# K's weights in 128-byte runs turned by VectorE, new PSUM banks for the first step, and a reordered tail in a conditioned-attention kernel

## The chip, the cores and the metric

The kernel runs on one core of one Trainium2 chip. The metric is the device time of one execution in microseconds (us). TensorE (PE; its weight loads are shown as PEld), VectorE (DVE), ScalarE (ACT), GpSimd (POOL) and SyncE (SP) run side by side; here SP issues nearly all DMAs and ScalarE a few.

## The reference

The input x is 8 x 512 x 512 (batch, sequence, model width) and every batch has one conditioning row. There are 16 heads of 32. All is float32.

```python
Q = split_heads(x @ Wq.T + bq)          # K and V likewise
tQ = split_heads(tokens @ Wq.T + bq)    # tK likewise; tokens: one row per batch
scores = einsum('bhqd,bhkd->bhqk', Q + tQ, K + tK) / sqrt(32)
out = einsum('bhqk,bhkd->bhqd', softmax(scores), V)
return x + out.transpose(0, 2, 1, 3).reshape(B, S, 512)
```

## The kernel before, in words

**Steps.** A step `t` (0 to 31) is one batch and one group of four heads, 128 columns of the width. It has four stages, one per 128-row block `kc`. A stage of step t computes `exponentials(t, kc)`: TensorE puts minus the row maxima into four PSUM banks by a small bf16 matmul (L553) and adds the scores, keys in rows (L556), and ScalarE takes the exponential out of each bank (L567). The same stage computes scores, queries in rows, of one row block of the next step (`row_max`, L492). VectorE reduces their maxima (L483 for one head, L501 for two), and `denominators` (L511) lets ScalarE take exponentials of the same banks only to sum them. The rest of a stage is either half of a pair of projections of q, k or v for later steps (`first_products` and `other_products`, 7 products instead of 8 by combinations of 256-blocks, L396 and L399), or `weighted`, the values' product of the step before (L572). When all maxima of a step stand, `split_max` splits them into three bf16 parts (on GpSimd) and `transpose_max` turns them (L537) into `maxT`, which the next step's exponentials need.

**Banks.** PSUM has eight banks of 128 x 512. A row of `TURNS` says which bank each use of a stage takes: places 0 to 3 the exponentials, 4 to 7 the row maxima, and the projections a place that the exponentials have left. `advance` goes to the next row. Rows 0 to 7 repeat over the steps, 8 to 11 serve the last steps (`row(i)`), 12 to 16 the stages ahead of step 0. Step 0 uses rows 0 to 3.

**Order.** The order on each engine is that of the code (`manual_schedule`); DMAs of a queue go out in the order of the code as well. A DMA issue waits till its tile is free, and an instruction waits for the tiles that it reads.

**Start.** Four x tiles, Wq, Wk and Wv come in. Wq and Wk are loaded in rows (256 KB a piece, 2 KB a row) and turned by TensorE through PSUM (`transpose_w`, L259; copies L266 to L272). Wv is loaded in 16 pieces of 64 KB in runs of 128 bytes (`spread`, L215), placed so that VectorE's turn of 32 x 32 blocks (L713) completes the transpose. `project_qk_part` (L343) projects group 0 and 1 of q and k. `condition` (L650), `untranspose` (L637) and `condition_end` (L659, L665) make the conditioning rows `tok`, which `project_qk_end` adds (L356 for q on VectorE, L358 for k on ScalarE). GpSimd forms the combined blocks of weights (`combine_w`, L288 to L291). Then come five stages (rows 12 to 16) of row maxima for step 0 and the second pair of groups, then step 0.

**End.** Steps 29, 30 and 31 have no projections left. `part_of` computes part of a step's values product and stores or adds it in `parts` (L757 to L764). For steps 30 and 31 no separate denominators are computed: GpSimd and VectorE sum the exponentials in `acc` and `acc2` (`sum_of`, L834, L836), and `times_ones` (L582) sums over the rows on TensorE. `send` turns a result on VectorE (L628), GpSimd scales it and adds the residual (L629, L630), and SP stores it in four pieces (L633). The last step is turned by TensorE (L637, L941) and stored in two halves (L952), one by SP and one by ScalarE.

Of the kernel before, what the change touches and what calls it, by code (L numbers as in the profile page):

```python
# [17 lines left out]
def kernel(  # L18
# [84 lines left out]
    ]  # L103
    turn = [0]

# [6 lines left out]
        return psum[:, j : k + 1 : k - j, :]  # L112

    def advance():
        turn[0] = (turn[0] + 1) % 8 if turn[0] < 8 else turn[0] + 1

    count = [0]

# [16 lines left out]
    def spread(a, d):  # L135

        return a.rearrange("(f j) d -> j f d", j=BL)[:, :, d : d + BL]
# [67 lines left out]
    nc.scalar.dma_start(cond_sb[B : B + 1, :], bq.rearrange("(o d) -> o d", o=1))  # L205
    nc.scalar.dma_start(cond_sb[B + 1 : B + 2, :], bk.rearrange("(o d) -> o d", o=1))
    load_w("q", Wq, nc.sync, [0])
    load_w("k", Wk, nc.sync, [0])
    load_w("q", Wq, nc.sync, [1, 2, 3])
    load_w("k", Wk, nc.sync, [1, 2, 3])  # L210

    wv = ws["v"].rearrange("p c (f e) -> p c f e", e=BL)
    for cc in range(NC):
        for h in range(HG):
            nc.sync.dma_start(  # L215
                wv[h * BL : (h + 1) * BL, cc], spread(Wv, cc * P + h * BL)
            )
    bvb = const.tile([P, D], F32, tag="bvb", name="bvb")
    nc.sync.dma_start(bvb, bv.rearrange("(o d) -> o d", o=1).broadcast_to([P, D]))
    bvs = const.tile([P, G, BL], F32, tag="bvs", name="bvs")  # L220
# [31 lines left out]
        n: const.tile([P, NC, D], F32, tag=f"wT{n}", name=f"wT_{n}") for n in ("q", "k", "v")  # L252
    }

    def transpose_w(n, dc, pt, odd=None):

        odd = dc % 2 if odd is None else odd
        for cc in range(NC):
            nc.tensor.transpose(  # L259
                pt[:, cc * P : (cc + 1) * P], ws[n][:, dc, cc * P : (cc + 1) * P], ident  # L260
            )
        o = wT[n][:, :, dc * P : (dc + 1) * P]
        pv = pt.rearrange("p (c s) -> p c s", c=NC)
        if n == "q":
            if odd:
                nc.vector.tensor_scalar(o, pv, SCALE, None, ALU.mult)  # L266
            else:
                nc.scalar.activation(o, pv, AF.Copy, scale=SCALE)
        elif odd:
            nc.vector.tensor_copy(o, pv)  # L270
        else:
            nc.scalar.copy(o, pv)  # L272
# [202 lines left out]
    def row_max(t, qc):  # L475
        if t >= T:
            return
        open_max(t)
        for j in range(HG):
            row_scores(t, qc, j, banks(HG + j))  # L480
        if t < T - 2:
            for j in range(2):
                nc.vector.tensor_reduce(  # L483
                    nmax[t][:, qc, j : j + 1, 0], banks(HG + j), AX.X, ALU.max, negate=True
                )
        else:
            row_max_of(t, qc, 0, banks(HG, 2))
        row_max_of(t, qc, 1, banks(HG + 2, 2))
# [27 lines left out]
                accum_out=sums[t][:, qc, j, :],  # L516
            )

    def split_max(t):

        if t >= T:
            return
        m, sp = nmax[t], split[t % 2]
        rest = op.tile([P, NS, HG, 1], F32, tag="rest", name=f"rest_{t}")
        nc.gpsimd.tensor_copy(sp[:, :, :, 0:1], m)
        nc.gpsimd.tensor_tensor(rest, m, sp[:, :, :, 0:1], ALU.subtract)
        nc.gpsimd.tensor_copy(sp[:, :, :, 1:2], rest)
        nc.gpsimd.tensor_tensor(sp[:, :, :, 2:3], rest, sp[:, :, :, 1:2], ALU.subtract)

    maxT = {}  # L530

# [146 lines left out]
    for half in range(2):  # L678
        combine_x(0, half, nc.gpsimd)
    transpose_w("q", 0, bank(6), 1)  # L680
    transpose_w("k", 0, bank(3), 0)
    transpose_w("q", 1, bank(7), 1)
    pc = bank(5)
    BB = B + 2
# [13 lines left out]
    transpose_w("q", 3, bank(1), 1)  # L698
    for cc in range(NC):
        project_qk_part(0, "k", cc, pk)  # L700
    transpose_w("k", 1, bank(5), 0)
    condition("q", bank(6))
    transpose_w("k", 2, bank(3), 1)
    transpose_w("k", 3, bank(7), 0)
    condition_end("q", bank(1), nc.vector)
    project_qk_end(0, "q", pq)
    condition("k", bank(5))
    for cc in range(2):
        project_qk_part(1, "q", cc, bank(7))
    condition_end("k", bank(0), nc.gpsimd)  # L710
    project_qk_end(0, "k", pk)
    for cc in range(NC):
        nc.vector.transpose(wT["v"][:, cc, :], ws["v"][:, cc, :])  # L713
    for cc in range(2, NC):
        project_qk_part(1, "q", cc, bank(7))
    project_qk_end(1, "q", bank(7))
    for n in ("q", "k", "v"):
        combine_w(n)

    def nothing():  # L720
# [2 lines left out]

    turn[0] = 12
    row_max(0, 0)
    denominators(0, 0)
    project_qk(1, "k", banks(1))
    advance()
    row_max(0, 1)
    first_products("q", 0, 1, lambda: denominators(0, 1), nothing, 0, 1)  # L730
    advance()
    row_max(0, 2)
    other_products("q", 0, 1, lambda: denominators(0, 2), nothing, (0, 1))
# [8 lines left out]
    other_products("k", 0, 1, lambda: denominators(1, 0), nothing, (0, 2))  # L742
    turn_x(NC + 1)
    load_residual(0)
    turn[0] = 0


    parts = {}
# [28 lines left out]
    for t in range(T - 3):  # L777
        b, r = divmod(t, G)

        exponentials(t, 0)  # L780
        row_max(t + 1, 1)
        of = ((t - 1) // G + 1, (t - 1) % G)
        dens = lambda: denominators(t + 1, 1)
        if t:
            project_pair("q", *of, dens, nothing, 1 if r % 2 else (0, 3))
        else:
            first_products("v", 0, 0, dens, nothing, 3)
            turn_x(NC + 2)
            load_residual(1)
        turn_x(t + NC + 3)  # L790
        advance()

        exponentials(t, 1)
        row_max(t + 1, 2)
        dens = lambda: denominators(t + 1, 2)
        if t:
            dens()
            weighted(
                t - 1, banks(0), banks(1), lambda: combine_x(b + 1, r) if r < 2 else None
            )  # L800
        else:
            dens()
            other_products("v", 0, 0, nothing, nothing, (1, 0))
        advance()

        exponentials(t, 2)
        row_max(t + 1, 3)
        split_max(t + 1)
        dens = lambda: denominators(t + 1, 3)
        if t:  # L810
            project_pair("k", *of, dens, nothing, 1 if r % 2 else (0, 3))
        else:
            first_products("v", 0, 1, dens, nothing, 3)
            combine_x(1, 0)
        if t:
            load_residual(t + 1)
        advance()

        exponentials(t, 3)
        row_max(t + 2, 0)  # L820
        dens = lambda: denominators(t + 2, 0)

        def small():
            transpose_max(t + 1, banks(2 if r % 2 else 1))

        project_pair("v", *of, dens, small, 1 if r % 2 else (0, 2))
        advance()
# [44 lines left out]
    exponentials(t, 0)  # L872
    row_max(t + 1, 1)
    apart = masked(t - 1)
    part_of(t - 1, banks(0), [2])
    row(1)
    exponentials(t, 1)
    row_max(t + 1, 2)
    acc = room_for_sums(t)
    sum_of(t, acc, 1, nc.gpsimd)  # L880
    part_of(t - 1, banks(0), [3])
    spread_sums(apart, banks(1))
    den = denominators_of(t - 1, banks(1))
    row(2)
    exponentials(t, 2)
    row_max(t + 1, 3)
    split_max(t + 1)
    pa = banks(0)
    times_v(t, 0, pa)

    exponentials(t, 3, (1, 2, 3, 4))
    times_v(t, 1, pa)
    transpose_max(t + 1, bank(5), nc.vector.tensor_copy)
    times_v(t, 2, pa)
    for kc in (2, 3):
        sum_of(t, acc, kc, nc.vector)
    send_parts(t - 1, den)

    t = T - 1
    exponentials(t, 0, (6, 7, 1, 2))  # L900
    times_v(t - 1, 3, pa)
    exponentials(t, 1, (3, 4, 5, 6))
    pv = bank(7)
    times_v(t, 0, pv)
    exponentials(t, 2, (1, 2, 3, 4))
    times_v(t, 1, pv)
    pd = bank(5)
    times_ones(acc, pd, True, True)
    acc2 = room_for_sums(t)
    sum_of(t, acc2, 1, nc.vector)  # L910
    den = op.tile([P, NB, BL], F32, tag="dead", name=f"den_{t - 1}")
    nc.vector.transpose(den.rearrange("p f e -> p (f e)"), pd)
    rec = op.tile([P, NB, 1], F32, tag="recs", name=f"recs_{t - 1}")
    nc.vector.reciprocal(rec, den[:, :, 0:1])
    send(t - 1, pa, rec)
    exponentials(t, 3, (6, 1, 2, 3))
    times_v(t, 2, pv)
    pd = bank(4)
    times_ones(acc2, pd, True, False)
    times_ones([es[t, 2, pr] for pr in range(NP)], pd, False, False)  # L920
    times_ones([es[t, 3, pr] for pr in range(NP)], pd, False, True)
    times_v(t, 3, pv)

# [3 lines left out]
    two = [slice(0, HS), slice(HS, S)]  # L927
    nc.vector.tensor_copy(oT[:, two[0]], pv[:, two[0]])
    nc.scalar.copy(oT[:, two[1]], pv[:, two[1]])
    pi, po = bank(2), [bank(6), bank(1)]  # L930
    untranspose(den, pi)
    rec = op.tile([P, NS, HG, 1], F32, tag="rec", name="rec")
    nc.vector.reciprocal(
        rec, pi.rearrange("p (c h e) -> p c h e", c=NS, h=HG)[:, :, :, 0:1]
    )
    y = op.tile([P, NS, P], F32, tag="res", name="res")
    b, g = divmod(t, G)
    for i in range(2):
        cs = slice(i * 2, i * 2 + 2)
        for qc in (i * 2, i * 2 + 1):  # L940
            nc.tensor.transpose(  # L941
                po[i][:, qc * P : (qc + 1) * P], oT[:, qc * P : (qc + 1) * P], ident
            )
        nc.vector.tensor_tensor(
            y[:, cs].rearrange("p c (h e) -> p c h e", h=HG),
            po[i][:, two[i]].rearrange("p (c h e) -> p c h e", c=2, h=HG),
            rec[:, cs].broadcast_to([P, 2, HG, HD]),
            ALU.mult,
        )
        last = (nc.gpsimd, nc.vector)[i]  # L950
        last.tensor_tensor(y[:, cs], y[:, cs], xr[t][:, cs], ALU.add)
        (nc.sync, nc.scalar)[i].dma_start(  # L952
            out[b].rearrange("(c p) d -> p c d", p=P)[:, cs, g * P : (g + 1) * P], y[:, cs]
        )

# [30 lines left out]
```

## Time and profile before

| | before |
|---|---|
| runs | 734.62 us median of 3 (734.4 to 734.93) |
| profiled execution | 734.58 us, span of the instructions 732.6 us, granted TensorE clock 0.999 |
| TensorE busy | 725.0 us, 99% of the span |
| ScalarE, VectorE, GpSimd busy | 619.1, 530.4 and 183.2 us |
| DMA | 29.64 MB, mean 40 GB/s |

The time of the profiled execution is its span and about 2.0 us around it. Matmuls are pipelined and their ends are modelled, so a busy TensorE is not one at its peak. A row of a timeline gives start and length in us, the engine, the line, the operation, what it writes and reads, and in brackets how long the engine had been idle and what ended that. A row of the chain gives start, length and the work that the end of the program goes back to.

### The profile page before, as it was taken

How to read it: one execution, taken by the hardware profiler on the slowest of the kernel's cores; microseconds unless marked ns; L12 is line 12 of the kernel's file. 1: busy time of each engine (PE TensorE's matmuls, PEld its weight loads, DVE VectorE, ACT ScalarE, POOL GpSimd, SP SyncE). 2: the span in 40 equal slices, each digit the busy share in tenths (PEclk: the TensorE clock that was granted, in tenths of full speed). 3: DMA queues.
4: the chain of work that ended last, by engine and by line, in shares of the span. 5: the costliest groups of instructions: out<-in, count | busy, mean ns of one | idle time of the engine just before them, and what ended most of it. 6: DMA issues, size and time to landing. Idle time of an engine off the chain costs nothing.

```text
span 732.6 us, 15105 instructions
## 1 busy us (share of the span) xinstructions
PE 725.0 (99%) x5416; PEld 402.8 (55%) x5416; DVE 530.4 (72%) x845; ACT 619.1 (85%) x1542; POOL 183.2 (25%) x282
## 2 busy tenths in 40 slices
PE   9999999999999999999999999999999999999997
PEld 5466555565555565555565555565555566555432
DVE  3697776777767877777776877777767777767666
ACT  2478988989988988988989888988988989898665
POOL 3622221122221122221122221122221122221373
PEclk9999999999999999999999999999999999999999
DMA  8524211212211212221212221212110111110112
GB/s 220 87 44 73 45 30 30 44 30 46 44 31 29 44 30 44 45 33 27 45 29 45 44 36 24 45 30 44 30 24 8 30 29 30 30 26 7 27 15 44
DMA packets 202142, 29.64 MB, mean 40 GB/s; under 512 B 199370, under 2 KB 200394, under 8 KB 202068
## 3 DMA queue, kind: packets, MB, share of 16 engines
q1 hardware_dynamic: 201488, 28.01, 23.5%
q8 instruction: 42, 0.69, 0.4%
q10 hardware_dynamic: 580, 0.68, 0.3%
q14 instruction: 32, 0.26, 0.1%
HBM read 20.27 MB, written 8.39 MB: 39 GB/s over the span
## 4 chain that ended last, share of the span: by engine, by line
PE 97%; ACT 1%; DMA 1%; DVE 1%; issue 0%; SPq 0%; POOL 0%; DVEq 0%; POOLq 0%
PE psum L399 26%; PE psum L572 16%; PE psum L492 15%; PE psum L556 15%; PE psum L396 14%; PE psum L553 6%; PE psum L343 2%; PE psum L537 1%; DMA w_k<-in_L_cond_Wk_dram 1%; ACT e L567 1%; PE psum L259 0%; PE psum L582 0%; DVE nmax L501 0%; PE psum L650 0%; PE psum L603 0%
## 5 line engine op out<-in xcount | busy, mean ns | idle before, releaser
L511 ACT ACTIVATE dead<-psum,nmax 128x512 f32<-128x512 f32 x480 | 327.6, 703 | 5.6 <-DVE nmax L483 3.6
L567 ACT ACTIVATE e<-psum 128x512 f32<-128x512 f32 x512 | 264.5, 603 | 77.8 <-PE psum L556 77.7
L483 DVE TENSOR_REDUCE nmax<-psum 128x1 f32<-128x512 f32 x240 | 154.6, 686 | 143.7 <-PE psum L492 143.7
L501 DVE TENSOR_REDUCE nmax<-psum 128x2 f32<-128x1024 f32 x136 | 164.7, 1216 | 10.4 <-PE psum L492 9.1
L629 POOL TENSOR_TENSOR res<-res,recs 128x512 f32<-128x512 f32 x31 | 33.4, 1077 | 447.1 <-DVE res L628 447.1
L492 PE MATMUL psum<-kT,qT 32*128 32x512 f32 x1024 | 136.4, 601 | 0.0
L556 PE MATMUL psum<-qT,kT 32*128 32x512 f32 x1024 | 132.9, 588 | 0.0
L572 PE MATMUL psum<-e,v 128*32 128x512 f32 x1024 | 120.5, 597 | 0.0
L511 ACT ACTIVATION_READ_ACCUMULATOR dead<-psum,nmax 128x1 f32 x480 | 105.3, 219 | 0.0
L492 PEld LDWEIGHTS psum<-kT,qT 32*128 32x128 f32 x1024 | 57.7, 183 | 56.8 <-ACT dead L511 22.2
L572 PEld LDWEIGHTS psum<-e,v 128*32 128x32 f32 x1024 | 26.3, 110 | 65.3 <-issue 37.7
L553 PE MATMUL psum<-maxT,onesb 3*128 3x512 bf16 x512 | 52.5, 384 | 0.0
L556 PEld LDWEIGHTS psum<-qT,kT 32*128 32x128 f32 x1024 | 51.0, 185 | 2.5 <-issue 0.2
L396 PE MATMUL psum<-wc_v,xc 128*128 128x256 f32 x192 | 49.5, 380 | 0.5 <-ACT e L567 0.5
L553 PEld LDWEIGHTS <-onesb 3*128 3x128 bf16 x512 | 13.4, 90 | 61.6 <-issue 51.9
L399 PE MATMUL psum<-xc,wc_k 128*128 128x256 f32 x180 | 46.2, 379 | 0.0
L399 PE MATMUL psum<-xc,wc_q 128*128 128x256 f32 x180 | 46.2, 379 | 0.0
L169 POOL TENSOR_TENSOR xr<-xr,bvs 128x512 f32<-128x512 f32 x31 | 39.4, 1272 | 18.2 <-DMA xr<-in_x_dram 18.1
L630 POOL TENSOR_TENSOR res<-res,xr 128x512 f32<-128x512 f32 x31 | 40.3, 1301 | 2.4
L396 PEld LDWEIGHTS psum<-wc_v,xc 128*128 128x128 f32 x192 | 36.3, 190 | 6.1 <-ACT e L567 1.3
L396 PE MATMUL psum<-wT_v,xT 128*128 128x256 f32 x128 | 38.7, 405 | 0.0
L399 PEld LDWEIGHTS psum<-xc,wc_k 128*128 128x128 f32 x180 | 34.2, 190 | 4.6
(153 smaller groups left out, 773.7 us busy)
## 6 DMA issues: line engine op xcount, KB each, us to landing
xr<-in_x_dram SPq DMA_DIRECT2D x124, 64.0 KB, 2.5
out_dram<-res SPq DMA_DIRECT2D x124, 64.0 KB, 2.0
x<-in_x_dram SPq DMA_DIRECT2D x112, 64.0 KB, 2.4
w_q<-in_L_cond_Wq_dram SPq DMA_DIRECT2D x4, 256.0 KB, 4.5
w_k<-in_L_cond_Wk_dram SPq DMA_DIRECT2D x4, 256.0 KB, 4.4
w_v<-in_L_cond_Wv_dram SPq DMA_DIRECT2D x16, 64.0 KB, 3.3
x<-in_x_dram ACTq DMA_DIRECT2D x2, 256.0 KB, 4.1
x<-in_x_dram SPq DMA_DIRECT2D x2, 256.0 KB
```

The costliest lines, as they stand in the source:

```text
L169: nc.gpsimd.tensor_tensor(xr[t], xr[t], bias, ALU.add)
L396: nc.tensor.matmul(pt, xb, w, start=(kc == kcs[0]), stop=(kc == kcs[-1]))
L399: nc.tensor.matmul(pt, w, xb, start=(kc == kcs[0]), stop=(kc == kcs[-1]))
L483: nc.vector.tensor_reduce(nmax[t][:, qc, j : j + 1, 0], banks(HG + j), AX.X, ALU.max, negate=True)
L492: nc.tensor.matmul(pt, qkT["q", t][r, qc * P : (qc + 1) * P], qkT["k", t][r, :], start=True, stop=True,)
L501: nc.vector.tensor_reduce(nmax[t][:, qc, pr * 2 : pr * 2 + 2, 0], pt, AX.X, ALU.max, negate=True)
L511: nc.scalar.activation(dead, banks(HG + j), AF.Exp, bias=nmax[t][:, qc, j, :], accum_out=sums[t][:, qc, j, :],)
L553: nc.tensor.matmul(bank[j], onesb[r, :], maxT[t][r, :], start=True, stop=False)
L556: nc.tensor.matmul(bank[j], qkT["k", t][r, kc * P : (kc + 1) * P], qkT["q", t][r, :], start=False, stop=True,)
L567: nc.scalar.activation(e[:, i, :], bank[pr * 2 + i], AF.Exp)
L572: nc.tensor.matmul(pt[j * HD : (j + 1) * HD, :], vs[b % 2][:, kc, (g * HG + j) * HD : (g * HG + j + 1) * HD], es[t, kc, j // 2][:, j % 2, ...
L630: nc.gpsimd.tensor_tensor(y, y, xr.pop(t), ALU.add)
```

## The change

1. **K's weights.** Only K's first 128 rows are still loaded in rows, into a tile of their own (`wk0`), and turned by TensorE. The other 384 columns of the transposed K come in 16 pieces of 48 KB in runs of 128 bytes, ahead of V's 16 pieces in SP's queue, and VectorE turns them in four instructions of 128x384. TensorE's 12 transposes of K and their three copies go.
2. **q's second group** (group 1) is projected in pieces: one quarter after `condition("q")`, one after `condition("k")`, two later; before, two and two after `condition("k")`.
3. **V's turns.** VectorE turns one quarter of V where it turned all four; the other three follow the maxima of row block 0. GpSimd's combination of V comes after them, still behind q's and k's.
4. **Banks.** Step 0 gets rows of its own (17 to 20 of `TURNS`), reached by `advance`, which then goes on with row 4. Its first products use place 1 instead of 3, its other products places (0, 2) instead of (1, 0). In row 13 the first products of q use place 0 for the first and place 1 for the second product instead of the reverse.
5. **Tail.** Step 29's two last parts are computed together in the first stage of step 30, with one copy and one addition fewer. Step 30's first block goes to `parts` and the other three are added by VectorE, its `send` reads `parts`. The last split of maxima is done by VectorE, and the last row block reduces its first two heads singly. GpSimd sums only one half of the first two exponentials of step 30. `acc2` also takes in the third block of step 31, so one `times_ones` of four matmuls goes. The last result has a tile of its own, and both of its stores are issued by ScalarE.

```diff
+        (0, 1, 2, 3, 4, 5, 6, 7),
+        (2, 4, 3, 5, 0, 1, 6, 7),
+        (0, 1, 4, 5, 2, 3, 6, 7),
+        (2, 4, 3, 5, 6, 7, 0, 1),
...
-        turn[0] = (turn[0] + 1) % 8 if turn[0] < 8 else turn[0] + 1
+        turn[0] = {7: 0, len(TURNS) - 1: 4}.get(turn[0], turn[0] + 1)
...
-    load_w("k", Wk, nc.sync, [0])
+    wk0 = op.tile([P, D], F32, tag="dead", name="wk0")
+    nc.sync.dma_start(wk0, Wk[:P, :])
     load_w("q", Wq, nc.sync, [1, 2, 3])
-    load_w("k", Wk, nc.sync, [1, 2, 3])
-    wv = ws["v"].rearrange("p c (f e) -> p c f e", e=BL)
-    for cc in range(NC):
-        for h in range(HG):
-            nc.sync.dma_start(
-                wv[h * BL : (h + 1) * BL, cc], spread(Wv, cc * P + h * BL)
-            )
+    for n, w, f in (("k", Wk, HG), ("v", Wv, 0)):
+        wn = ws[n].rearrange("p c (f e) -> p c f e", e=BL)
+        for cc in range(NC):
+            for h in range(HG):
+                nc.sync.dma_start(
+                    wn[h * BL : (h + 1) * BL, cc, f:], spread(w, cc * P + h * BL)[:, f:]
+                )
...
-        if t < T - 2:
+        if t < T - 2 or t * NS + qc == T * NS - 1:
...
-    transpose_w("k", 1, bank(5), 0)
+    def turn_w(n, ccs, rows=slice(0, D)):
+        for cc in ccs:
+            nc.vector.transpose(wT[n][:, cc, rows], ws[n][:, cc, rows])
+
+    turn_w("k", range(NC), slice(P, D))
     condition("q", bank(6))
-    transpose_w("k", 2, bank(3), 1)
-    transpose_w("k", 3, bank(7), 0)
+    project_qk_part(1, "q", 0, bank(7))
     condition_end("q", bank(1), nc.vector)
     project_qk_end(0, "q", pq)
     condition("k", bank(5))
-    for cc in range(2):
-        project_qk_part(1, "q", cc, bank(7))
+    project_qk_part(1, "q", 1, bank(7))
     condition_end("k", bank(0), nc.gpsimd)
     project_qk_end(0, "k", pk)
-    for cc in range(NC):
-        nc.vector.transpose(wT["v"][:, cc, :], ws["v"][:, cc, :])
+    turn_w("v", [0])
...
-    for n in ("q", "k", "v"):
+    for n in ("q", "k"):
         combine_w(n)
...
     row_max(0, 0)
+    turn_w("v", [1, 2, 3])
+    combine_w("v")
...
-    first_products("q", 0, 1, lambda: denominators(0, 1), nothing, 0, 1)
+    first_products("q", 0, 1, lambda: denominators(0, 1), nothing, 1)
...
-    turn[0] = 0
+    advance()
...
-            first_products("v", 0, 0, dens, nothing, 3)
+            first_products("v", 0, 0, dens, nothing, 1)
...
-            other_products("v", 0, 0, nothing, nothing, (1, 0))
+            other_products("v", 0, 0, nothing, nothing, (0, 2))
...
-            first_products("v", 0, 1, dens, nothing, 3)
+            first_products("v", 0, 1, dens, nothing, 1)
...
-    part_of(t - 1, banks(0), [2])
+    part_of(t - 1, banks(0), [2, 3])
+    spread_sums(apart, banks(1))
+    den = denominators_of(t - 1, banks(1))
...
-    sum_of(t, acc, 1, nc.gpsimd)
-    part_of(t - 1, banks(0), [3])
-    spread_sums(apart, banks(1))
-    den = denominators_of(t - 1, banks(1))
+    sum_of(t, acc, 1, nc.gpsimd, [0])
+    part_of(t, banks(0), [0])
+    send_parts(t - 1, den)
...
-    split_max(t + 1)
-    pa = banks(0)
-    times_v(t, 0, pa)
+    split_max(t + 1, nc.vector)
+    pa, rest = banks(0), [1, 2, 3]
+    times_v(t, 1, pa, rest)
     exponentials(t, 3, (1, 2, 3, 4))
-    times_v(t, 1, pa)
+    times_v(t, 2, pa, rest)
     transpose_max(t + 1, bank(5), nc.vector.tensor_copy)
-    times_v(t, 2, pa)
-    for kc in (2, 3):
-        sum_of(t, acc, kc, nc.vector)
-    send_parts(t - 1, den)
+    sum_of(t, acc, 1, nc.vector, [1])
+    sum_of(t, acc, 2, nc.vector)
     t = T - 1
     exponentials(t, 0, (6, 7, 1, 2))
-    times_v(t - 1, 3, pa)
+    times_v(t - 1, 3, pa, rest)
+    nc.vector.tensor_tensor(parts[t - 1], pa, parts[t - 1], ALU.add)
+    sum_of(t - 1, acc, 3, nc.vector)
     exponentials(t, 1, (3, 4, 5, 6))
     pv = bank(7)
     times_v(t, 0, pv)
-    exponentials(t, 2, (1, 2, 3, 4))
+    acc2 = room_for_sums(t)
+    sum_of(t, acc2, 1, nc.vector)
+    exponentials(t, 2, (1, 2, 3, 0))
     times_v(t, 1, pv)
     pd = bank(5)
     times_ones(acc, pd, True, True)
-    acc2 = room_for_sums(t)
-    sum_of(t, acc2, 1, nc.vector)
+    sum_of(t, acc2, 2, nc.vector)
...
-    send(t - 1, pa, rec)
-    exponentials(t, 3, (6, 1, 2, 3))
+    send_parts(t - 1, den[:, :, 0:1])
+    exponentials(t, 3, (4, 6, 1, 2))
     times_v(t, 2, pv)
...
-    times_ones([es[t, 2, pr] for pr in range(NP)], pd, False, False)
...
-        (nc.sync, nc.scalar)[i].dma_start(
+        nc.scalar.dma_start(
```

More of the change, by code (lines that the diff above doesn't have):

```diff
@@ L253, with transpose_w @@
     }
-    def transpose_w(n, dc, pt, odd=None):
+    def transpose_w(n, dc, pt, odd=None, of=None):
         odd = dc % 2 if odd is None else odd
+        of = ws[n][:, dc, :] if of is None else of
         for cc in range(NC):
             nc.tensor.transpose(
-                pt[:, cc * P : (cc + 1) * P], ws[n][:, dc, cc * P : (cc + 1) * P], ident
+                pt[:, cc * P : (cc + 1) * P], of[:, cc * P : (cc + 1) * P], ident
             )
@@ L517, in denominators, with split_max @@
             )
-    def split_max(t):
+    def split_max(t, on=nc.gpsimd):
         if t >= T:
@@ L524, in split_max @@
         rest = op.tile([P, NS, HG, 1], F32, tag="rest", name=f"rest_{t}")
[L525 to L528, printed above, removed]
+        on.tensor_copy(sp[:, :, :, 0:1], m)
+        on.tensor_tensor(rest, m, sp[:, :, :, 0:1], ALU.subtract)
+        on.tensor_copy(sp[:, :, :, 1:2], rest)
+        on.tensor_tensor(sp[:, :, :, 2:3], rest, sp[:, :, :, 1:2], ALU.subtract)
     maxT = {}
@@ L680 @@
     transpose_w("q", 0, bank(6), 1)
-    transpose_w("k", 0, bank(3), 0)
+    transpose_w("k", 0, bank(3), 0, wk0)
     transpose_w("q", 1, bank(7), 1)
@@ L908 @@
     times_ones(acc, pd, True, True)
-    acc2 = room_for_sums(t)
-    sum_of(t, acc2, 1, nc.vector)
+    sum_of(t, acc2, 2, nc.vector)
     den = op.tile([P, NB, BL], F32, tag="dead", name=f"den_{t - 1}")
     nc.vector.transpose(den.rearrange("p f e -> p (f e)"), pd)
-    rec = op.tile([P, NB, 1], F32, tag="recs", name=f"recs_{t - 1}")
-    nc.vector.reciprocal(rec, den[:, :, 0:1])
-    send(t - 1, pa, rec)
-    exponentials(t, 3, (6, 1, 2, 3))
+    send_parts(t - 1, den[:, :, 0:1])
+    exponentials(t, 3, (4, 6, 1, 2))
     times_v(t, 2, pv)
-    pd = bank(4)
+    pd = bank(3)
     times_ones(acc2, pd, True, False)
-    times_ones([es[t, 2, pr] for pr in range(NP)], pd, False, False)
     times_ones([es[t, 3, pr] for pr in range(NP)], pd, False, True)
@@ L929 @@
     nc.scalar.copy(oT[:, two[1]], pv[:, two[1]])
-    pi, po = bank(2), [bank(6), bank(1)]
+    pi, po = bank(0), [bank(4), bank(6)]
     untranspose(den, pi)
@@ L935 @@
     )
-    y = op.tile([P, NS, P], F32, tag="res", name="res")
+    y = op.tile([P, NS, P], F32, tag="res_last", name="res", bufs=1)
     b, g = divmod(t, G)
```

## The prediction

> **What bounds the kernel now.** I read the busy shares first, then the chain that ended last, then the timelines of the first 48 us, of step 0 and of the last 25 us.
>
> ```profile
> span 732.6 us, 15105 instructions
> PE 725.0 (99%) x5416; PEld 402.8 (55%) x5416; DVE 530.4 (72%) x845; ACT 619.1 (85%) x1542; POOL 183.2 (25%) x282
> ...
> PE 97%; ACT 1%; DMA 1%; DVE 1%; issue 0%; SPq 0%; POOL 0%; DVEq 0%; POOLq 0%
> ```
>
> TensorE is the bound. From step 1 to step 28 nothing in the diff touches the order or the banks, so gains and losses arise before about 70 us and after about 699 us, and a shift made early carries through undamped. The chain, in order of time:
>
> ```profile
> 17.02 0.44 PE psum L259 x4
> 17.46 0.99 PE psum L650 x8
> 18.45 1.04 PE psum L259 x8
> ...
> 19.51 0.60 ACT wT_k L272
> ...
> 20.15 1.07 PE psum L650 x8
> 21.22 1.91 PE psum L343 x4
> 23.13 0.44 PE psum L637 x4
> 23.57 1.72 PE psum L343 x4
> 25.29 1.07 PE psum L492 x8
> ```
>
> See here that turning three quarters of K's weights (L259) costs TensorE 0.44 + 1.04 us, and that the condition product of K (L650 at 20.15) waits for ScalarE's copy of the last quarter.
>
> ```profile
> 31.51 1.13 PE L399 MATMUL psum<-xT,wT_q 128*128 128x256 f32 x4 [0.45 <-ACT kT L358]
> ...
> 51.19 1.13 PE L396 MATMUL psum<-wc_v,xc 128*128 128x256 f32 x4 [0.23 <-ACT e L567]
> ...
> 55.97 1.13 PE L396 MATMUL psum<-wT_v,xc 128*128 128x256 f32 x4 [0.31 <-ACT e L567]
> ```
>
> These timeline rows are almost all of TensorE's open waits: a bank that ScalarE still reads. And the source of the small pieces, and of the tail:
>
> ```profile
> 8.15 10.96 SPq L215 DMA_DIRECT2D w_v<-in_L_cond_Wv_dram  x16
> ...
> 23.89 2.49 DVE L713 STREAM_TRANSPOSE wT_v<-w_v 128x512 f32<-128x512 f32 x4
> ...
> 713.05 4.62 DVE L836 TENSOR_TENSOR acc<-acc,e 128x1024 f32<-128x1024 f32 x4
> ...
> 718.33 3.18 DVE L834 TENSOR_TENSOR acc<-e,e 128x1024 f32<-128x1024 f32 x2
> ```
>
> **Part 1, K turned by VectorE.** TensorE loses 12 transposes and ScalarE and VectorE lose three copies of some 0.6 us; VectorE gains four turns of 128x384, each three quarters of 2.49/4, so 0.47 us. TensorE's path from 17.02 was 8.27 us (the rows above). After, it is condition q 0.99, one quarter of q's second group (1.91 + 1.72)/4 = 0.91, untranspose 0.44, condition k 1.07, a quarter 0.91, untranspose 0.44, two quarters 1.72: 6.48. Gain 1.79; I take 1.7, as pieces restarted after a wait run a little longer.
>
> Condition: K lies turned when condition k is due, at 17.02 + 0.99 + 0.91 + 0.44 = 19.36, so its last piece must land by 19.36 - 0.47 - 0.1 = 18.8. SP issues 16 pieces where three 256 KB loads stood, from the same 6.48. The nearest row is V's: 10.96/16 = 0.685 us each, but 0.487 is the median of one issue, and the long ones (up to 1.53) mostly follow the three K loads that are now gone; the four bvs issues took 1.85, 0.46 each. So the last issue is between 6.48 + 0.83 + 14 x 0.5 = 14.3 (the second waits till 7.31, as its row did) and 6.48 + 15 x 0.685 = 16.8; landing takes 2.6 to 4.8, median 3.3. That is 16.9 to 21.6. I take 15 + 3.3 = 18.3, nearest to the medians: on time by 0.5. At 21.6, 2.8 us would be lost. What is queued behind these turns on VectorE: sum_q, tok, q's exit, sum_k, V's first turn, the row maxima; behind condition k on TensorE, everything.
>
> Here a rule speaks against the change. The Trainium skill, "DMA: Bandwidth & Descriptors", sections "Specifications" and "Rules for kernel authors", wants at least 512 B for line rate and says to coalesce small transfers; "Anatomy of one DMA" gives about 2.0 us fixed per DMA. One after another, 16 pieces would be an estimated 32 us, K would land near 38, and the kernel would be 20 us slower, at 754. The V row decides: 16 pieces of 128-byte runs were issued in 10.96 us with 2.6 to 4.8 us to landing each, so they overlap. A second rule, "VectorE: DVE Perf Modes", section "Rules for kernel authors", gives 128x128 transposes to TensorE where PSUM will do. In engine time that is right (1.48 against 1.88 us, and +0.4 if the engines were alike), but VectorE is idle from 14.4 to 19.15, with 4.8 before L270.
>
> **What is pushed back.** In SP's queue V's 16 pieces, bvb, bvs and the next batch's 16 x pieces start some 7 us later. V's last piece: 15.5 + 10.96 - 0.5 + 3.3 = 29.3 (ends 27 and 32.5). Its three late turns on VectorE (1.87 us) stand ahead of the maxima of row block 1, ready near 29.3. TensorE needs those banks only after 3.29 us of products, and a maximum plus exponential for two heads takes about 2.3 us, so up to about 1 us of lateness is hidden; at 32.5 some 2 us would not be. I take 0. x's pieces landed by 31.8 and are first turned at 43.87: 10 us of cover. GpSimd does wc_q and wc_k first (about 10 us from 22.6), so wc_v, now last, ends near 37.5 against 39.4 before, needed after 45. K's first quarter has its own tile, same size and place in the queue: 0.
>
> **Part 2, banks of the prologue and step 0.** First products of q go to bank 7, so the 0.45 wait on L358 falls: -0.45. Each stage of a step begins with L553, so the chain gives their lengths:
>
> ```profile
> 47.85 0.33 PE psum L553 x4
> ...
> 53.62 0.33 PE psum L553 x4
> ...
> 59.26 0.33 PE psum L553 x4
> ...
> 65.02 0.33 PE psum L553 x4
> ...
> 70.56 0.33 PE psum L553 x4
> ...
> 75.83 0.33 PE psum L553 x4
> ```
>
> Step 0 has 5.77, 5.64, 5.76 and 5.54 us. The next stage, with equal work, has 5.27 (70.56 to 75.83). Excess of the first three: 0.50 + 0.37 + 0.49 = 1.36. The new rows put the second product on the bank of the second exponential, not the fourth. What could be late next is ScalarE: 2.07 for the exponentials, 4 x 0.67 for the denominators, 0.4 for a copy, 5.2 of 5.27. I take -1.25; bounds -1.36 and -0.3.
>
> **Part 3, the tail.** TensorE does one times_ones less: -0.86. Two value products of step 29 move into one stage, which leaves its 3.6 us rhythm (scores 1.02, maxima 2.36 on VectorE) and grows by about 0.5; the last stage loses as much. Row maxima and split end where they did: maxima 0.5 later, four small VectorE instructions (0.2 each with their waits) for GpSimd's 1.27. Transposes of the maxima at 712.28 as before, but no product hides the copy after them: exps of step 31 start at 713.25 instead of 713.60, so -0.35. Then VectorE: nine adds at 4.62/4 = 1.14 (contended 1.6) and one of 0.65 from PSUM, in a row from 713.1, end at 724.0. The parts add waits for the last value product (715.4, done before its turn); behind it queue both accumulators. times_ones(acc2) is due at 722.9 and waits 1.1 us. So of 0.35 + 0.86 some 0.2 to 0.3 is left at TensorE's end. The normalised step 30 is then later: den, reciprocal and turn till 725.5, GpSimd 1.05 + 1.28 till 728.0, SP's four stores till 729.9, landing about 731.4; ScalarE's two stores go out at 729.05 and 729.5, one behind the other, against 729.64 for the last before. I take -0.2; bounds -0.9 (no wait on VectorE) and +0.6 (contended adds).
>
> **Sum.** -1.7 - 0.45 - 1.25 - 0.2 = -3.6 us. The profiled execution took 734.58 us (span 732.6 and 2.0 around it), 0.04 under the median of the runs, 734.62: 731.0.
>
> **Rivals.**
> A, slower: K's small pieces arrive late. It costs 1 us per us after 18.8, and turns the sum positive by 0.2% (1.5 us) from a landing at 23.9. If every piece took the long issue (the mean of the two longest neighbours, 0.96 and 1.53, is 1.25): last issue 25.2, landing 28.5, 9.7 lost, 740.7. For it: 128-byte runs moved at 76 to 126 GB/s in the windows from 12 to 20 us, against 351 to 388 from 6 to 10 us, where the big ones ran. Against it: no large loads lie ahead any more after 9.3. Chance 0.06.
> B, partly late: K or V by 1 to 3 us: 732 to 734. Chance 0.10.
> C, VectorE bounds the tail: contended adds as at 718.33 (1.59 each): tail +0.6, 731.8. For: ten instructions in a row. Against: GpSimd is idle then. Chance 0.12.
> D, the banks don't do it: ScalarE's 5.2 us stay the limit of step 0, only 0.3 gained: 732.0. Chance 0.10.
> Forecast: 0.62.
>
> **Numbers.** A measurement of this kernel can tell about 0.2% from no change, 1.5 us. Forecast, C and D lie wholly below 733.1, and half of B: 0.89 faster, 0.06 same, 0.05 slower, after a little of B and A goes to same. The range takes the forecast's bounds (-4.5) and goes up over C, D and the first half of B: 730.2 to 732.9.
>
> **What would show it.** Right: no L259 on K after 8.7 us, TensorE without a wait at condition k, row scores of block 0 near 23.6, the first L553 near 45.7, step 0's stages near 5.3, and a wait of times_ones on the accumulator near the end. Wrong: condition k or sum_q waiting on w_k's landing, maxima of block 1 behind V's turns with TensorE idle, or exponentials again ahead of products in step 0's chain.

## The result and the profile after

| | before | after |
|---|---|---|
| median of 9 runs | 734.93 us (734.4 to 736.12) | 732.68 us (732.33 to 734.05) |
| ratio | | 0.9974, 95% interval 0.9965 to 0.9982 |
| profiled execution | 734.58 us, span 732.6 | 734.05 us, span 732.3 |
| TensorE busy | 725.0 us | 722.3 us |

The kernel became faster by 2.25 us (by 1.94 against the 734.62 us from which the forecast started), where 3.6 were forecast. TensorE's busy time fell by 2.7 us, and its share of the span is still 99%. The profiled execution of after is one of two of the nine at 734.05, with a late start (the wait of 1.19 us below); the execution of the same kernel in the experiments (`again`, 732.62 us, span 730.8, a wait of 0.22) is nearer to the median, and the readings below use both.

The page and the chain of waits of after, in the order in which they were shown of before (start us, length us, work):

```profile
span 732.3 us, 15085 instructions
PE 722.3 (99%) x5396; PEld 401.8 (55%) x5396; DVE 535.7 (73%) x857; ACT 617.7 (84%) x1540; POOL 177.0 (24%) x276
```

```profile
9.16 1.19 issue
10.35 0.39 PE psum L693 x4
10.74 3.63 PE psum L350 x8
...
18.68 0.99 PE psum L657 x8
...
21.16 1.00 PE psum L657 x8
...
23.65 1.72 PE psum L350 x4
25.37 1.07 PE psum L499 x8
...
47.42 0.33 PE psum L560 x4
52.69 0.33 PE psum L560 x4
58.04 0.33 PE psum L560 x4
63.30 0.33 PE psum L560 x4
68.95 0.33 PE psum L560 x4
74.22 0.33 PE psum L560 x4
...
721.10 1.23 DVE acc L847
722.37 1.48 PE psum L589 x10
```

See four things. From the condition product of q (L657 at 18.68) to the first row scores (L499 at 25.37) the path is 6.69 us; before, from the transposes of K that stood at its head, it was 8.27, and 6.48 was forecast. K's condition product starts without a wait. The stages of step 0 are 5.27, 5.35, 5.26 and 5.65 us, where they were 5.77, 5.64, 5.76 and 5.54. In the tail, `times_ones` (L589) waits for VectorE's last addition to `acc2` (L847), as forecast. But the transposes of the condition rows (L693) start after a wait, which the profile before did not show. The timeline of VectorE has K's turns, on time, and the row of additions in the tail, without a gap and at the uncontended 1.14 us each:

```profile
15.96 2.03 DVE L711 STREAM_TRANSPOSE wT_k<-w_k 128x384 f32<-128x384 f32 x4
...
28.80 1.89 DVE L711 STREAM_TRANSPOSE wT_v<-w_v 128x512 f32<-128x512 f32 x3
31.16 1.29 DVE L490 TENSOR_REDUCE nmax<-psum 128x1 f32<-128x512 f32 x2 [0.48 <-PE psum L499]
...
717.69 2.35 DVE L845 TENSOR_TENSOR acc<-e,e 128x1024 f32<-128x1024 f32 x2
719.96 2.35 DVE L847 TENSOR_TENSOR acc<-acc,e 128x1024 f32<-128x1024 f32 x2
722.23 0.70 DVE L925 STREAM_TRANSPOSE den<-psum 128x512 f32<-128x512 f32 x1
```

So the engines did in the tail what was forecast: taken from the start of step 30, VectorE's last operation (L961) ends 0.2 us earlier than before. What comes behind it is the surprise. Before, the last two stores were issued at 729.35 and 729.64, and the span ended 3.0 us after the end of VectorE's last operation (729.61):

```profile
729.35 0.40 SPq L952 DMA_DIRECT2D out_dram<-res  x1
729.64 0.42 ACTq L952 DMA_DIRECT2D out_dram<-res  x1
...
out_dram<-res SPq DMA_DIRECT2D x1, 128.0 KB, 1.9
```

In after, the timeline, and behind it the view of the DMAs from 719 to 735 us in 40 slices of 0.4 us (busy tenths of the 16 engines, GB/s, then KB each and the median us from issue to landing), show the end like this:

```profile
726.37 2.04 SPq L640 DMA_DIRECT2D out_dram<-res  x4
...
727.07 0.63 DVE L961 TENSOR_TENSOR res<-res,xr 128x256 f32<-128x256 f32 x1
...
727.45 1.04 ACTq L962 DMA_DIRECT2D out_dram<-res  x2
```

```profile
DMA  0000000000000000000037777988900000000000
GB/s 0 0 0 0 0 0 0 0 0 0 0 0 0 0 0 0 0 0 0 0 54 109 119 109 119 269 130 171 245 7 0 0 0 0 0 0 0 0 0 0
...
out_dram<-res SPq DMA_DIRECT2D x4, 64.0 KB, 2.6
out_dram<-res ACTq DMA_DIRECT2D x2, 128.0 KB, 3.2
```

VectorE is done at 727.70 and the halves are issued at 727.45 and 727.98, but the second one (the trace has no landing of the first) lands 3.2 us after its issue instead of 1.9 to 2.0, and the span ends 4.6 us after VectorE. Step 30's four stores, in runs of 128 bytes, are issued from 1.1 us ahead of them and between them: the DMA engines are busy from 727.0 to 730.6 without a gap, first at some 115 GB/s, then with both sets.

### The profile page after: what moved, and what is told of

It reads as the page before. It is cut to its first block, busy times and chain, and to the rows that moved or that the text cites. A ratio compares the mean times of both kernels' runs of the same rounds, so it can differ in the third digit from the quotient of the medians.

```text
span 732.3 us, 15085 instructions
## 1 busy us (share of the span) xinstructions
PE 722.3 (99%) x5396; PEld 401.8 (55%) x5396; DVE 535.7 (73%) x857; ACT 617.7 (84%) x1540; POOL 177.0 (24%) x276
## 4 chain that ended last, share of the span: by engine, by line
PE 96%; DVE 2%; issue 1%; DMA 1%; SPq 0%; DVEq 0%
PE psum L406 26%; PE psum L499 16%; PE psum L579 15%; PE psum L563 14%; PE psum L403 14%; PE psum L560 6%; PE psum L350 2%; PE psum L544 1%; DMA x<-in_x_dram 1%; DVE acc L847 1%; PE psum L266 0%; DVE acc L845 0%; PE psum L657 0%; PE psum L589 0%; PE psum L610 0%
## 5 line engine op out<-in xcount | busy, mean ns | idle before, releaser
L499 PE MATMUL psum<-kT,qT 32*128 32x512 f32 x1024 | 136.4, 601 | 0.0
L499 PEld LDWEIGHTS psum<-kT,qT 32*128 32x128 f32 x1024 | 58.1, 183 | 56.2 <-ACT dead L518 23.1
L406 PEld LDWEIGHTS psum<-xc,wc_q 128*128 128x128 f32 x180 | 34.2, 190 | 4.7
```

The lines of the kernel that those rows point to most:

```text
L406: nc.tensor.matmul(pt, w, xb, start=(kc == kcs[0]), stop=(kc == kcs[-1]))
L499: nc.tensor.matmul(pt, qkT["q", t][r, qc * P : (qc + 1) * P], qkT["k", t][r, :], start=True, stop=True,)
```

## Experiments

Two theories for the missing 1.3 us. **S**: step 30's late stores and the last two collide. **H**: the head (start and banks) brings less than forecast. Times are against runs of the kernel before on the same chip, whose median was 734.78 us in the first set, 735.13 in the second and 734.55 in the third; each set ran on another chip. The ratios with their intervals are those on record, and not quotients of the two medians.

**First set: the change in two halves, and the end without the stores.** `again` is the kernel after, unaltered.

> The changed kernel unaltered, for a second profile. Theory S (stores): its last two halves leave 1.6 to 1.9 us earlier than before on TensorE's and VectorE's side, but step 30's four stores run beside them and landing takes 3.1 us instead of 1.9, so it is 2.0 to 2.5 us faster than before, and the profile again shows the last landing more than 3 us after its issue. The 1.2 us wait for the conditioning row at 9.2 us in the first profile is a matter of that one execution and will be absent. Theory H (head): the late start belongs to the change (small pieces in the DMA engines beside the small rows of the biases), and this profile shows that wait too, with the store side secondary.

`head` has the new start and the new banks with the tail of before (in the diff, - is the kernel after):

```diff
-    times_v(t - 1, 3, pa, rest)
-    nc.vector.tensor_tensor(parts[t - 1], pa, parts[t - 1], ALU.add)
-    sum_of(t - 1, acc, 3, nc.vector)
+    times_v(t - 1, 3, pa)
...
-        nc.scalar.dma_start(
+        (nc.sync, nc.scalar)[i].dma_start(
```

> The new start and the new banks with the tail of before. Theory S: the start and step 0 give what was forecast for them, 3.4 us, so 3.1 to 3.6 us faster than before, and about 1.1 us faster than the whole change. Theory H: the start gives only about 2 us, so 1.8 to 2.4 us faster than before, the same as the whole change within 0.4.

`tail` is the reverse, the new tail on the start and banks of before:

```diff
-    turn_w("k", range(NC), slice(P, D))
+    transpose_w("k", 1, bank(5), 0)
...
-            first_products("v", 0, 0, dens, nothing, 1)
+            first_products("v", 0, 0, dens, nothing, 3)
```

> The tail of the change on the start and banks of before. Theory S: 0.9 to 1.4 us slower than before, as TensorE's and VectorE's gain of 0.2 is outweighed by stores that collide at the end. Theory H: 0.2 us faster than before, as the forecast had it.

`nostore` is the kernel after without the four stores of step 30, so that block of the output is not written:

```diff
-        for h in range(HG):
+        for h in range(HG if store else 0):
...
-        send(t, parts[t], rec)
+        send(t, parts[t], rec, t != T - 2)
```

> The changed kernel with the four stores of step 30 left out; everything that computes it stays. That step's block of the output is not written. Theory S: the two last halves land 1.9 us after their issue again, and the kernel is 1.1 to 1.4 us faster than the changed one. Theory H: the end was set by the halves' own issue, so at most 0.3 us faster.

| run | us (range) | against before | ratio, 95% interval |
|---|---|---|---|
| `again` | 732.41 (732.18 to 732.62) | -2.37 | 0.9964 (0.9951 to 0.9976) |
| `head` | 731.96 (731.3 to 732.54) | -2.82 | 0.9957 (0.9945 to 0.997) |
| `tail` | 735.58 (735.18 to 737.08) | +0.80 | 1.0011 (1.0002 to 1.0019) |
| `nostore` | 731.1 (730.73 to 733.56) | -3.68 | 0.9945 (0.9931 to 0.9958) |

The new tail by itself makes the kernel slower, where the prediction had -0.2 us; S expected a little more, 0.9 to 1.4. `head` lies between the two theories. Without the four stores the kernel is 1.31 us faster than `again`, within what S expected. The view of the DMAs over the same window shows why; first `nostore`:

```profile
GB/s 0 0 0 0 0 0 0 0 0 0 0 0 0 0 0 0 0 0 0 0 0 0 0 0 0 0 223 231 202 0 0 0 0 0 0 0 0 0 0 0
...
out_dram<-res ACTq DMA_DIRECT2D x2, 128.0 KB, 1.9
```

and `again`, the timeline and then the DMAs:

```profile
725.22 2.29 SPq L640 DMA_DIRECT2D out_dram<-res  x4
...
726.30 1.18 ACTq L962 DMA_DIRECT2D out_dram<-res  x2
```

```profile
GB/s 0 0 0 0 0 0 0 0 0 0 0 0 0 0 0 0 0 36 127 100 110 117 249 283 229 83 0 0 0 0 0 0 0 0 0 0 0 0 0 0
```

The two halves alone (0.26 MB) are moved in three slices, 1.2 us. In `again` the same halves come while the four stores, also 0.26 MB, are under way, and together they take from 725.9 to 729.3. The second half lands 2.6 us after its issue (S expected over 3), and the last landing is a store of step 30, issued at 726.76 and landed at 729.73. In both traces the first half is issued 29.9 us after the start of step 30, and from that start the span ends after 34.42 us in `again` and 33.19 in `nostore`: all of the difference lies behind the issue. H has a part too: `head` brought 2.82 us, where its terms were -1.7, -0.45 and -1.25, together 3.4.

`tail` tests the forecast of the end directly, for its step 30 starts only 0.16 us later than before's:

```profile
728.23 1.95 SPq L633 DMA_DIRECT2D out_dram<-res  x4
...
729.31 0.95 ACTq L951 DMA_DIRECT2D out_dram<-res  x2
```

The forecast had the four issues done by 729.9 (they end at 730.18) and the halves issued at 729.05 and 729.5 (729.31 and 729.83), all within 0.35 us. It had the landing at about 731.4; the second half landed at 731.94 and the last of the four stores at 732.79.

**Second set: the stores moved out of the way, the wait at the start, and two terms of the head.** `es2` is the kernel after, but `acc2` does not take in step 31's third block, so VectorE reaches step 30's `send` two additions earlier:

```diff
-    sum_of(t, acc2, 2, nc.vector)
...
+    times_ones([es[t, 2, pr] for pr in range(NP)], pd, False, False)
```

> The changed kernel, but acc2 does not take in the third block of step 31: VectorE has two additions of 1.14 us less ahead of step 30's send, and TensorE sums that block itself again (one times_ones of four matmuls, 0.86 us). Theory S (at the end the last two stores land late because step 30's four stores were issued just ahead of and beside them): the send starts 2.3 us earlier, so step 30's stores are out of SP's queue by about 725.2 and the two last stores, issued near 725.9 and 726.4, land 1.9 us after their issue and not 2.6 to 3.2; TensorE gains 0.4 on its own (0.86 more work, against waits of acc2 of 1.2 in all): -1.3 to -1.7 against the changed kernel, -3.7 to -4.1 against the kernel before. Rival (the two last stores are slow because both are in ScalarE's queue, one behind the other): only the 0.4 on TensorE is gained, -2.8 against before. Rival (TensorE bounds the end): +0.86, -1.5 against before.

731.29 us (731.26 to 731.44), -3.84 against before, ratio 0.995 (0.9937 to 0.9962). The timeline and the view of the DMAs:

```profile
723.17 2.04 SPq L640 DMA_DIRECT2D out_dram<-res  x4
...
726.13 0.95 ACTq L962 DMA_DIRECT2D out_dram<-res  x2
```

```profile
DMA  0000000000003778791078700000000000000000
GB/s 0 0 0 0 0 0 0 0 0 0 0 0 54 110 118 122 118 133 22 0 209 236 211 0 0 0 0 0 0 0 0 0 0 0 0 0 0 0 0 0
...
out_dram<-res ACTq DMA_DIRECT2D x2, 128.0 KB, 1.9
```

The two sets of transfers are apart: 2.4 us for the stores, a gap, and 1.2 us for the halves, of which the second again lands 1.9 us after its issue. From the start of step 30 the span ends after 33.06 us, 1.36 less than in `again`; 0.38 of that is the halves' earlier issue, and about 1.0 their landing. Both halves are still in ScalarE's queue, so the rival that blames that queue falls. TensorE does 0.86 us more and the kernel is still faster, so TensorE's `times_ones` was not what bounded the end.

`best` is `es2` with the transposes of the condition rows behind q's first four products:

```diff
+    pq, pk = bank(4), bank(2)
+    for cc in range(NC):
+        project_qk_part(0, "q", cc, pq)
     pc = bank(5)
...
             pc[:, cc * BB : (cc + 1) * BB], cond_sb[:, cc * P : (cc + 1) * P], ident[:BB, :BB]
```

> As es2, and besides TensorE's four small transposes of the conditioning rows come after the first four products of q instead of ahead of them, so that the last of those rows (bk) has 3.7 us more to land. Theory: the wait of 0.2 us in front of them in the changed kernel goes (and that of 1.1 to 1.2 in the executions that started late): -0.2 us against es2, and no executions 1.5 us above the others. Rival (the start is bound elsewhere, by VectorE's and ScalarE's copies for the products, and the wait only covers them): the same time as es2.

730.84 us (730.75 to 731.16), -4.29, ratio 0.9944 (0.9931 to 0.9956): 0.45 under `es2`, where 0.2 was expected, and the ranges do not touch. TensorE's timeline of `es2` has the wait, that of `best` has none:

```profile
9.39 0.38 PE L693 MATMUL psum<-ident,cond_sb 10*128 10x10 f32 x4 [0.45 <-issue]
```

```profile
8.65 3.60 PE L350 MATMUL psum<-xT,wT_q 128*128 128x512 f32 x8
12.19 0.41 PE L696 MATMUL psum<-ident,cond_sb 10*128 10x10 f32 x4
```

`banks` is the kernel before with nothing but the new rows of banks:

```diff
-            first_products("v", 0, 0, dens, nothing, 3)
+            first_products("v", 0, 0, dens, nothing, 1)
...
-    turn[0] = 0
+    advance()
```

> The kernel before with nothing but the new rows of banks (step 0's own rows, and the places of its products and of q's first products). Forecast's terms: -0.45 for the bank wait and -1.25 for step 0's first three stages, so -1.7 us, stages of 5.3, 5.3 and 5.3 us where they were 5.8, 5.6 and 5.8. With the head as a whole at -2.8 this leaves -1.1 for K turned by VectorE. Rival (the banks don't carry it, and K does): -0.8, stages above 5.5.

733.44 us (733.17 to 734.13), -1.69, ratio 0.998 (0.9971 to 0.9989). Its chain has 5.26, 5.35 and 5.27 us for the first three stages of step 0:

```profile
48.58 0.33 PE psum L558 x4
...
53.84 0.33 PE psum L558 x4
...
59.19 0.33 PE psum L558 x4
...
64.46 0.33 PE psum L558 x4
```

That is the forecast sum of -1.7, with an interval of some 0.7 us to either side. In the trace, from the first row scores to step 0 0.51 us went, and the 0.45 us wait is gone; the first three stages of step 0 gave 1.29, of which the fourth took 0.10 back. Of the head's 2.82 this leaves 1.13 us for K.

`klate8` puts eight of V's pieces ahead of K's sixteen:

```diff
-    for n, w, f in (("k", Wk, HG), ("v", Wv, 0)):
+    for n, w, f, ccs in (("v", Wv, 0, [0, 1]), ("k", Wk, HG, range(NC)), ("v", Wv, 0, [2, 3])):
...
-        for cc in range(NC):
+        for cc in ccs:
```

> The changed kernel with the first eight of V's small pieces ahead of K's sixteen in SP's queue; nothing else moves. K's last piece lands 4.3 us later, near 21.3 where it landed at 16.9, VectorE's last turn of K ends near 22.0, and the product of K with the conditioning rows was due at 19.9. If the price past the slack of 2.3 us is one to one: +2.0 to +2.3 us against the changed kernel, near 0 against the kernel before. If pieces land earlier by less queueing, or later work takes the wait up: under +1. If V's pieces, whose runs are longer, slow K's more: over +3.

735.85 us (735.0 to 736.81), +0.72 against before, ratio 1.0009 (1.0 to 1.0018), and so 3.1 us slower than the kernel after, taking `again`'s -2.37 for that. The timeline:

```profile
20.13 1.69 PE L657 MATMUL psum<-wT_k,condT 128*32 128x512 f32 x6
...
22.52 0.58 DVE L711 STREAM_TRANSPOSE wT_k<-w_k 128x384 f32<-128x384 f32 x1 [1.79 <-DMA w_k<-in_L_cond_Wk_dram]
...
23.15 1.05 PE L657 MATMUL psum<-wT_k,condT 128*32 128x512 f32 x2 [1.33 <-DVE wT_k L711]
```

The last turn ends at 23.10 and the condition product was due at 20.13: 2.97 us late, 3.1 us of time. The price is one to one, as rival A of the prediction had it. What was sized wrong is the lateness: K's last piece landed at 22.40, 5.5 us later than in `again` (16.94) and not 4.3, since one issue among K's last pieces took 1.4 us; `again` has such a one too, at 16.13, but among V's. The last piece itself landed 2.3 us after its issue (2.4 in `again`), so V's pieces, which are larger (64 KB against 48, in runs of 128 bytes like K's), did not slow it. In `again` the last turn ends at 17.64 for a product due at 19.99, so the slack was 2.3 us, not the 0.5 forecast.

**Third set: a last gain, whose wait it was, and half of the stores.** `best_b` repeats `best`.

> The kernel of the run best once more, as the measure for best2 on the same chip: -4.1 to -4.4 us against before.

730.69 us (730.54 to 730.89), -3.86, ratio 0.9947 (0.9934 to 0.9959). `best2` adds the scores ahead of the maxima in step 31's first stage:

```diff
-            nc.tensor.matmul(bank[j], onesb[r, :], maxT[t][r, :], start=True, stop=False)
+                nc.tensor.matmul(
+                    bank[j], onesb[r, :], maxT[t][r, :], start=first, stop=not first
+                )
...
+        last = t == T - 1 and kc == 0
+        if not last:
+            less_max(True)
...
+        if last:
+            less_max(False)
```

> As best, and in the first stage of step 31 TensorE adds the scores first and minus the row maxima after them, so that the scores cover the 0.52 us for which it waits for VectorE's copy of the turned maxima. Theory (TensorE's own work sets its end in the tail): -0.4 to -0.5 us against best. Rival (the end of the tail hangs on VectorE's row of additions and step 30's stores, which now come 0.5 nearer to the last two): 0 to -0.2.

730.47 us (730.29 to 730.59), -4.08, ratio 0.9943 (0.9931 to 0.9956). The wait of 0.52 us is gone from its timeline, and the time fell by 0.22, near the rival's bound. The traces show where much of the rest went: two stages later `times_ones` on `acc` takes 1.28 us where it took 1.11 in `best_b`, because VectorE's addition ahead of it ends only at 715.92, after TensorE has got there (715.75).

`condfirst` makes `best`'s move of the condition rows on the kernel before (the diff is that of `best`).

> The kernel before with nothing but the four small transposes of the conditioning rows moved behind the first four products of q. It asks whose the late bk row is. If K's small pieces in the new order of loads make that row late (the changed kernel waits 0.2 to 0.45 us for it, the kernel before did not in its profile): the same as before, within 0.2. If the old order has that wait as well in most executions: -0.4 to -0.5, and the shortfall of the start against the forecast has another cause.

734.36 us (734.17 to 734.52), -0.19, ratio 0.9995 (0.9987 to 1.0004): the same as before. The interval does not exclude 0.4 us, but the traces of `before` and `tail` show no wait there either (that of `banks` does, in an execution with a late start). So the usual execution of the kernel before does not seem to lose time on that row, and the changed one does.

`two` leaves out only the last two of step 30's four stores, so half of that block is not written:

```diff
-        for h in range(HG):
+        for h in range(hs):
...
-        send(t, parts[t], rec)
+        send(t, parts[t], rec, 2 if t == T - 2 else HG)
```

> The changed kernel with only the first two of step 30's four stores, so that half of that block is not written. Between the changed kernel (-2.4 against before) and nostore (-3.7). If what counts is that the last of the four is issued beside the two last stores and lands 3 us later: nearly all of the 1.3 is back, -3.4 to -3.7. If every store of 128-byte runs ahead takes its share of the engines that move them: half, -3.0 to -3.1.

731.42 us (731.07 to 732.68), -3.13, ratio 0.9955 (0.9941 to 0.9969). It lies between `again` and `nostore`, as it should if every store takes its share; its second half landed 2.1 us after its issue. From the start of step 30 the span ends after 33.61 us, between 34.42 and 33.19. The intervals overlap both neighbours, so it leans to the share and does not settle it.

## Why the prediction was right and where it was wrong

**Direction and bound: right.** TensorE is the bound, and what is gained in the head is carried through: from the start of step 1 to that of step 30 the traces take 628.74 us before and 628.66 in after.

**The banks (-0.45 and -1.25): right**, -1.69 measured alone, with 0.51 and 1.18 in its trace.

**K turned by VectorE (-1.7): right in its mechanism, 0.6 too large.** The path fell by 1.6 us in the trace (8.27 to 6.69). The term put at nothing is a wait ahead of that path, at the transposes of the condition rows: 0.22 us in `again` and 0.45 in `es2`. The row of `bk`, issued by ScalarE at 5.6 to 5.9 us, is the last of what they read. Moving them back by four products gave 0.45 (`best`); the same move gave -0.19, the same as before, on the kernel before (`condfirst`). The traces give no landing of that row; its packet, taken to be the last of 2 KB in ScalarE's queue at the start, ends at 8.3 to 8.4 us in `again`, `head` and `es2` and at 7.7 in `before` and `tail`, but at 7.7 in `best2` too, which has the new order. So that the new order of loads makes the row late is likely and not shown, and that K's small pieces, issued from 6.9 us on, delay it on the DMA engines is a guess. The margin of K itself was forecast at 0.5 us with a landing at 18.3; it landed at 16.94 and had 2.3. The 2.0 us that the prediction took from the Trainium skill, "DMA: Bandwidth & Descriptors", section "Anatomy of one DMA", are given there for DMAs that GpSimd issues, so its 32 us did not describe SP's queue; the sixteen pieces took 10.1 us from the first issue to the last landing in `again`.

**V behind K (0): right.** V's late turns end at 30.69 and the maxima of row block 1 follow at 31.16, with TensorE not waiting.

**The tail (-0.2): wrong, and this is the step that failed.** Its engine part held: adds uncontended, `times_ones` on `acc2` waiting, VectorE's end 0.2 us earlier. The failed term is the landing: "SP's four stores till 729.9, landing about 731.4; ScalarE's two stores go out at 729.05 and 729.5, one behind the other, against 729.64 for the last before". The text saw the two sets of stores beside each other, gave the four the landing that they have alone, compared the halves with before by their issue, and put nothing on what the sets cost each other. Alone a half lands 1.9 to 2.0 us after its issue; together it took 2.6 to 3.2, and the last of the four 3.0 to 3.1. `nostore` prices it at 1.31 us; with it the tail is +0.80 alone (`tail`) and +0.45 on the new head (`again` against `head`), where -0.2 was forecast. The Trainium skill, "DMA: Bandwidth & Descriptors", section "Issuing engines are not separate DMA queues", says that DMAs started by different engines run on the same 16 engines and interleave; the slices of `again` and `es2` agree. The prediction had weighed that page's rule on small transfers for K, where the pieces overlap and their latency is hidden, and put it aside. The same page's "Specifications" want 512 bytes for line rate, and at the end of the kernel, where nothing hides a transfer, the rates of `es2` go with it: the stores in runs of 128 bytes moved at 110 to 133 GB/s, the halves in runs of 512 at 209 to 236. The stores are also smaller (64 KB against 128) and come from 32 partitions each instead of 128, and no run changed the length of the runs alone.

**The sum.** By the medians the -2.37 of `again` is banks -1.69, K -1.13 and tail +0.45. The split adds up by construction; K is the difference of `head` and `banks`, which ran on two chips, the tail that of `again` and `head` on one chip, and each is uncertain by half a us or more. The traces, one execution each, give the same head: in `again` the first row scores start 1.09 us earlier than before (24.13 against 25.22), step 0 1.61 earlier (46.18 against 47.79) and step 1 2.78 earlier (67.71 against 70.49). They give a dearer tail: from the start of step 30 to the end of the span it is 33.33 us before, 34.41 in `tail` and 34.42 in `again`, so +1.1. Against -3.6, K was taken 0.6 too large, and the tail was wrong by 0.65 (medians) to 1.3 (traces). `nostore` is 0.86 under `head` in the medians and 0.32 in the traces (33.19 against 33.51); such a difference is of the size of the scatter of `head`'s own runs, 731.3 to 732.54.

**A better version.** Putting `times_ones` back, moving the condition rows and turning the order of the first accumulation around (`best2`) makes 730.47 us, 0.9943 of before (0.9931 to 0.9956), against 0.9964 to 0.9974 for the change as it was.

## What to carry to other kernels

At the end of a kernel a store has no cover, and stores from different queues share the engines that move them: add up the moving time of everything that is issued close to the end (its bytes by the rate that such a store reaches in the profile), and let the slow block go out a full moving time (here 2.4 us) ahead of the last one. An operation taken off the bounding engine can cost more than it saves if the engine that takes it on then releases such a store late: here 0.86 us of TensorE against 1.3 us. And when loads ahead of a small row are made smaller or moved, look up the row's first reader, even if nothing in the change touches it.

## What the hardware showed unexpectedly

The order of two issues 0.2 us apart went together with a microsecond of waiting. In the profiles with a wait of 0.45 us or less, ScalarE issues the row of `bq` 0.2 us ahead of SP's third piece of Wq (in `again` at 4.64 against 4.82); in the four profiles with a wait of 1.1 to 1.3 us on the condition rows (after, `banks`, `nostore`, `two`) it comes 0.2 us behind it (in after at 4.88 against 4.69):

```profile
4.69 1.69 SPq L183 DMA_DIRECT2D w_q<-in_L_cond_Wq_dram  x2
...
4.88 0.23 ACTq L210 DMA_DIRECT2D cond_sb<-in_L_cond_bq_dram  x1
6.39 0.23 ACTq L211 DMA_DIRECT2D cond_sb<-in_L_cond_bk_dram  x1
```

It happens with the old head too (`banks`). No run set the order on purpose, so this is a coincidence in ten profiles and not a shown cause. With the transposes moved back (`best`, `best_b`, `best2`) no run is more than 0.4 us above the fastest of its kernel. And SP's small pieces go out every 0.51 us (K's sixteen in 8.17 us), land 2.1 to 3.5 us after their issue in `again` with several under way at once, and now and then one issue holds the queue for 1.4 us or more (1.56 in `again`).
